# A front in written order, a last projection by output, and means added to x1: one change to a Mamba block with linear attention behind it

## The chip, the cores and the metric

The kernel runs on one core of one Trainium2 chip. A core has five engines that work side by side: TensorE (PE) multiplies matrices into PSUM, VectorE (DVE), ScalarE (ACT) and GpSimd (POOL) work on SBUF and, but for GpSimd, on PSUM, and SyncE (SP) here only issues DMA transfers; ScalarE issues some as well. Each engine takes its instructions in order, and waits on semaphores for the others. The metric is the device time of one execution in microseconds (us). The kernel before takes 7801.51 us, the median of 3 runs (7790.71 to 7805.82).

## The reference

The input `x` is float32, 4 images of 512 channels and 64 x 64 positions (L = 4096). Two layers are added to it:

```python
# layer 0, on gn(x): group norm over 32 groups of 16 channels
xn = layer_norm(xf, norm_g, norm_b)                  # over the 512 channels
chunks = xn cut into 4 blocks of 128 channels, each a sequence of its own
xz = chunks @ in_proj_w.T;  xi, z = split(xz)        # 256 + 256
xc = silu(depthwise_conv4(xi) + conv_b)
dt, Bs, Cs = split(xc @ x_proj_w.T)                  # 8, 16, 16
dt = softplus(dt @ dt_proj_w.T + dt_proj_b)
h[t] = exp(dt*A) * h[t-1] + (dt*xc)[:, None] * Bs    # 256 x 16 states, 4096 steps
y = sum over states of h * Cs + xc * D;  y = y * silu(z)
ym = y @ out_proj_w.T + skip * chunks
x1 = x + layer_norm(ym) @ proj_w.T + proj_b
# layer 1, on gn(x1): linear attention, 8 heads of 64
q, k, v = split(gn(x1) @ w_qkv.T + b_qkv);  q, k = relu(q), relu(k)
kq = sum over positions of k q';  norm = kq.sum + 1e-6
out = x1 + (v kq / norm) @ w_out.T + b_out
```

## The kernel before

**Tiles and steps.** An image is cut into 8 tiles of T = 512 positions, and a tile into 4 chunks of 128 channels: 4 x 8 x 4 = 128 steps (b, t, c). A step makes the projections of its chunk (`inputs`: `pc` for the convolved half through four shifted products with `w_cv`, `pz` for z), `dt`, B and C (`mixers`: `pd`, then `parts`, a bf16 copy of B and C with corrections), the softplus of `dt` (`time_banks`, `time_steps`), and the product `u = dt * xc`. `dt` and `u` (both in one tile `both`, called dt in the profile) are written to DRAM row by row (`to_rows`: `d_rows`) and read back spread out (`spread`: `d_all`), so that 128 partitions hold 4 states of 32 channels: 32 rows, 4 slots `j`, four times over for the states. B is read back as `b_all`, the last 128 columns of C as `c_sb`; the other 384 columns of C are spread by a product with `sel` into PSUM (`c_all`).

**The scan loop.** A step has SLOTS = 16 slots of two scans each. In a slot, GpSimd makes the products `bx = u * B` for two scans (`drive`, L806, two slots ahead), ScalarE the decays `dA = exp(dt * A)` (`decay`, L798, three scans ahead, into three PSUM banks), VectorE the scans (`slot`, L824), every second slot VectorE multiplies the states by C (L844) and GpSimd the last quarter of them (L836), and TensorE sums over the states (`fold_states`). Between them the loop's planner puts the pieces of the next steps' projections, of the next tile's norms (`ahead`), of the tile just scanned (`late`: second norm and projection to x1) and of the attention of the image before (`rest`), each at a slot written by hand or by due times. This loop runs under `tc.manual_schedule()`: its instructions stand in each engine's queue in the order in which the code makes them. What stands before and after the loop is put in order by the framework's own scheduler.

**The front.** Before the loop, ScalarE's queue issues the loads of all weights and biases, `w_pr` (1 MB, the last projection) and `w_qk` (2 MB) among them. Preparations follow in the code: `w_cv` (L234), `dg` (L264), the bias rows `bqk` (L287 to L291), `a_k` and 16 small DMAs on SP that lay it out as `a_t` (L295 to L300), and the folding of the norm's weights into `w_pr`: offsets `pw` (L313), scaling by g (L315), centring by column means (`pw_mean`, L321) and `about` (L331). Then `input_norm(0)`: `stats0` loads the image's 8 tiles into a ring of three buffers (L148) and takes their statistics (L885), `stats_end` makes mean and deviation. `tile_norm(0, 0)` loads the first tile a second time, into `xn` (L519), and applies group norm and layer norm (`normed`, `group_norm`, `layer_norm`). Step 0 then goes through `step_inputs`, `silu`, `mixers`, `time_steps`, `to_rows` and `spread`, step 1 through the first three of these, and the first two products and three decays are made.

**After the loop.** The last tile's projection is `projected_last`: statistics of `ym` by TensorE while the last chunk finishes, 16 products `pp` over 4 outputs `o` and 4 chunks `c` with `c` as the outer loop, and on VectorE for each output the scaling (`sq`, L599), the sum with offset and x (`xr`, L600), its statistics (L603) and their aggregate (L341). The last image's attention follows with nothing beside it: `pq` and `pk` over all positions, then `m2` (`pm` of `w_o` and `kqn`), `m3 = w_v m2 * gr` with the identity added (L1040), the offsets `pob` = m2 bv + m3 ngm with `ngm` the negative group means (and `bo` lessened by `ngm`, since the identity is in m3), and for each tile 16 products `pr = m3 x1`, evicted with the offset `ob` (L1101) and stored. Loaded tiles `xa`, `xb`, `w_o`, `w_v` share one ring of three buffers.

## Time and profile before

| | us |
|---|---|
| median of 3 runs | 7801.51 |
| the profiled execution | 7798.74 |
| its span, first to last instruction | 7797.0 |
| busy: DVE, POOL, PE, ACT | 6968.4, 6892.5, 6424.5, 5442.5 |
| statistics of the first image end (aggregate begins) | 53.4 |
| first product `bx` begins | 114.6 |
| first scan begins | 117.0 |
| last `mv_last` aggregate begins | 7389.8 |
| first product `pr` of the last attention begins | 7678.7 |

A line of a timeline gives the start and the length in us, the engine (SPq and ACTq are their DMA queues, PEld is the loading of TensorE's weights), the line of the code, the operation, what it writes and reads, how often, and in brackets how long the engine had been idle and what released it. Where a helper makes the instruction, its line is the helper's (L129 for all products), and the tile's name tells which it is. One float32 product is two records of TensorE. A table by stretch gives for each stretch the busy time of each engine in turn, then PEclk, the share of full clock granted to TensorE, the DMA engines' busy share, and GB/s.

### The profile page before, as it was taken

The numbers are of one execution on the slowest core, as the hardware profiler recorded it, in microseconds if no ns is written. First come the engines' busy times: TensorE is split into PE (matmuls) and PEld (weight loads), VectorE is DVE, ScalarE is ACT, GpSimd is POOL, SyncE is SP. The second block draws the span as 40 slices with busy tenths as digits, with TensorE's granted clock in tenths as the row PEclk, the third lists the DMA queues.
The fourth block names the chain that finished last, engine by engine and source line by source line (L and its number), as shares of the span: only waits on it lengthen the run. The fifth ranks groups of instructions, "written<-read, shape, count | busy, mean of one in ns | idle before, by whom it ended". The sixth has DMA issues, their size and how long they took to land.

```text
span 7797.0 us, 90419 instructions
## 1 busy us (share of the span) xinstructions
PE 6424.5 (82%) x24816; PEld 2092.9 (27%) x24816; DVE 6968.4 (89%) x5784; ACT 5442.5 (70%) x8289; POOL 6892.5 (88%) x4637
## 2 busy tenths in 40 slices
PE   5677777677789888987788889898788888899699
PEld 1121211111223222332222223332122322333144
DVE  5999999999999999999999999999999999999720
ACT  4667777777777777777777777777777777777421
POOL 4999999999999999999999999999999999999700
PEclk8888888888899999999899999999899999999799
DMA  5666666666666666776766666677666666677402
GB/s 164 165 171 164 158 152 164 162 163 167 173 177 163 162 165 165 181 197 170 174 163 178 177 159 160 165 189 191 162 168 162 159 156 151 159 199 193 126 33 92
DMA packets 829327, 1266.37 MB, mean 162 GB/s; under 512 B 183928, under 2 KB 317576, under 8 KB 816528
## 3 DMA queue, kind: packets, MB, share of 16 engines
q1 hardware_dynamic: 805408, 1223.89, 61.2%
q0 software_dynamic: 16368, 32.51, 2.4%
q8 instruction: 194, 3.18, 0.2%
q10 hardware_dynamic: 7040, 4.20, 0.2%
q14 instruction: 317, 2.60, 0.1%
HBM read 1053.30 MB, written 206.57 MB: 162 GB/s over the span
## 4 chain that ended last, share of the span: by engine, by line
DVE 34%; PE 30%; ACT 10%; DMA 9%; issue 8%; POOL 6%; SPq 3%; DVEq 0%; POOLq 0%; ACTq 0%
DVE h L824 21%; DVE h L844 10%; PE y L129 6%; PE pc L129 6%; PE pq L129 5%; POOL bx L806 5%; DMA d_all<-d_rows 4%; ACT dA L798 3%; PE pr L129 3%; PE po L129 3%; SPq L773 3%; DMA c_sb<-c_rows 2%; PE pp L129 2%; DVE xn L421 2%; PE c_all L129 1%
## 5 line engine op out<-in xcount | busy, mean ns | idle before, releaser
L806 POOL TENSOR_TENSOR bx<-d_all,b_all 128x1024 f32<-128x1024 f32 x2048 | 4824.0, 2367 | 195.2 <-DVE h L824 175.0
L824 DVE TENSOR_TENSOR_SCAN h<-dA,st,bx 128x512 f32<-128x512 f32 x3584 | 4353.8, 1263 | 289.1 <-PE y L129 106.9
L798 ACT ACTIVATE dA<-d_all,a_t 128x512 f32<-128x512 f32 x4096 | 2759.3, 688 | 1503.8 <-DVE h L824 1447.3
L844 DVE TENSOR_TENSOR h<-h,c_all 128x1536 f32<-128x1536 f32 x1024 | 1767.2, 1726 | 0.1
L836 POOL TENSOR_TENSOR h<-h,c_sb 128x512 f32<-128x512 f32 x1024 | 1299.7, 1269 | 97.7 <-DMA c_sb<-c_rows 12.0
L129 PE MATMUL y<-h,fold 128*32 128x512 f32 x8192 | 1264.7, 693 | 50.1 <-POOL h L836 48.4
L129 PE MATMUL c_all<-parts,sel 128*128 128x384 bf16 x1024 | 367.5, 359 | 1021.7 <-DVE h L844 1020.8
L129 PE MATMUL pc<-xn,w_cv 128*128 128x512 f32 x2048 | 1036.5, 640 | 118.8 <-DVE xn L421 57.4
L129 PE MATMUL pq<-w_qk,xa 128*128 128x512 f32 x2048 | 960.2, 604 | 2.5 <-ACT xa L379 2.5
L824 DVE TENSOR_TENSOR_SCAN h<-dA,bx 128x512 f32<-128x512 f32 x512 | 590.3, 1202 | 74.3 <-POOL bx L806 50.9
L129 PEld LDWEIGHTS pc<-xn,w_cv 128*128 128x128 f32 x2048 | 386.4, 199 | 731.2 <-issue 409.5
L129 PEld LDWEIGHTS <-sel 128*128 128x128 bf16 x1216 | 120.3, 99 | 1654.7 <-DVE h L844 1445.6
L129 PEld LDWEIGHTS pq<-w_qk,xa 128*128 128x128 f32 x2048 | 392.7, 195 | 441.7 <-issue 425.9
L129 PE MATMUL pp<-xn,w_pr 128*128 128x512 f32 x1024 | 478.1, 596 | 0.0
L129 PE MATMUL pr<-xb,m 128*128 128x512 f32 x1024 | 476.1, 603 | 2.2 <-ACT res L1101 1.6
L129 PE MATMUL y<-xz,dg 32*32 32x512 f32 x2048 | 357.5, 775 | 0.0
L129 PEld LDWEIGHTS y<-h,fold 128*32 128x32 f32 x8192 | 170.5, 114 | 640.5 <-issue 385.2
L866 POOL TENSOR_TENSOR xz<-xz 128x512 f32<-128x512 f32 x256 | 325.2, 1270 | 8.1 <-ACT xz L863 7.2
L713 POOL TENSOR_TENSOR dt<-dt,xz 128x1024 f32<-128x1024 f32 x128 | 302.2, 2361 | 19.7 <-ACT dt L705 19.7
L129 PE MATMUL pd<-xz,w_xp 128*128 128x512 f32 x512 | 286.9, 687 | 5.2 <-ACT xz L1172 5.2
L129 PE MATMUL pz<-xn,w_z 128*128 128x512 f32 x512 | 270.5, 621 | 7.5 <-ACT xz L692 6.0
L129 PE MATMUL po<-xz,w_op 128*128 128x512 f32 x512 | 258.8, 628 | 5.2 <-POOL xz L866 5.0
(218 smaller groups left out, 5866.8 us busy)
## 6 DMA issues: line engine op xcount, KB each, us to landing
d_all<-d_rows SPq DMA_DIRECT2D x2048, 256.0 KB, 4.4
b_all<-b_rows SPq DMA_DIRECT2D x4096, 64.0 KB, 2.4
d_rows<-dt SPq DMA_DIRECT2D x256, 512.0 KB, 2.8
c_sb<-c_rows SPq DMA_DIRECT2D x4096, 16.0 KB, 3.6
xs<-in_x_dram SPq DMA_DIRECT2D x32, 1024.0 KB, 7.3
xn<-in_x_dram SPq DMA_DIRECT2D x32, 1024.0 KB, 8.3
x<-xr SPq DMA_DIRECT2D x32, 1024.0 KB, 4.3
xa<-x SPq DMA_DIRECT2D x32, 1024.0 KB, 7.0
```

The costliest lines, as they stand in the source:

```text
L129: nc.tensor.matmul(out_, lhsT, rhs, **how)
L421: nc.vector.tensor_tensor(v, v, bc(m, NC), op)
L713: nc.gpsimd.tensor_tensor(f["both"][:, 1], f["both"][:, 0], f["xz"][:, 0], ALU.mult)
L773: nc.sync.dma_start(dst[k * BLK : (k + 1) * BLK, :], rows_[q * KS + k, :].partition_broadcast(BLK))
L798: nc.scalar.activation(dAs[k], fs[n]["d_all", e][:, 0, j, :], AF.Exp, scale=a_t[:, e, j, q : q + 1])
L806: nc.gpsimd.tensor_tensor(bxs[g], fs[n]["d_all", e][:, 1, jj * 2 : jj * 2 + 2, :], bc(b_all[g // JJ], 2), ALU.mult)
L824: nc.vector.tensor_tensor_scan(h[:, j, :], dAs.pop(2 * g + i), bxs[g][:, i, :], 0.0 if t == 0 else st[:, c, e, q, j : j + 1], ALU.mult, AL ...
L836: nc.gpsimd.tensor_tensor(h[:, :, CUT:], h[:, :, CUT:], bc(c_sb.pop(g // JJ), NJ), ALU.mult)
L844: nc.vector.tensor_tensor(own, own, bc(c_all.pop(g // JJ), NJ), ALU.mult)
L866: nc.gpsimd.tensor_tensor(f["xz"][:, 1, e, :], f["xz"][:, 1, e, :], f["xz"][:, 0, e, :], ALU.mult)
```

## The change

The front, from the first weight to the last piece before the loop, now also runs under `tc.manual_schedule()`, so that its instructions stand in written order. Within it:

- The first tile is loaded straight into `xn`; `stats0` takes its statistics there, and `normed` doesn't load it again. `w_pr` and `w_qk` are issued by SP after the eighth x tile.
- The preparations become functions: `w_cv` is made between the statistics of the second and the third tile, the rest after the first group norm; the offsets `pw` are spread over the first tile's norm, and the centring of `w_pr` stands behind the decays.
- The tables of ScalarE's functions are loaded at written places.
- Step 1's `inputs` is begun before step 0's `mixers`. Step 0's softplus, `u`, and rows are made half by half (e = 0, 1); after the first half, `spread` by slot reads `d_all` in sixteen DMAs instead of eight, first the slots 0 and 1 of dt and of u, then 2 and 3. `c_sb` and the second and third `b_all` are issued behind them. Step 1's `mixers` comes after the first decays.

In `projected_last` the products run by output after the first chunk of all four. In the last image's attention the part `m3 ngm` of the offsets is left out; instead VectorE adds `ngm` to each tile of x1, 4 instructions per tile, and then m3 is applied to the sum.

```diff
@@ -164,6 +164,9 @@
+    front = ExitStack()
+    front.enter_context(tc.manual_schedule())
...
@@ -231,7 +234,10 @@
-    nc.vector.tensor_tensor(w_cv, conv_bc, w_x.unsqueeze(1).to_broadcast([P, NTAP, DI]), ALU.mult)
+    def prepare_conv():
+        nc.vector.tensor_tensor(w_cv, conv_bc, w_x.unsqueeze(1).to_broadcast([P, NTAP, DI]), ALU.mult)
...
@@ -269,9 +278,9 @@
-    w_pr = const_rows(proj_w, "w_pr")
+    w_pr = const.tile([P, NC, C], F32, tag="w_pr", name="w_pr")
-    w_qk = const_rows(wqk, "w_qk")
+    w_qk = const.tile([P, NC, 2 * C], F32, tag="w_qk", name="w_qk")
...
@@ -284,51 +293,60 @@
     bv = column(b_qkv[2 * C : 3 * C], NC, "bv")
     bo = column(b_out, NC, "bo")
+    def prepare_bias():
+        nc.vector.tensor_copy(bqk, b_qk)
+        for i in (2, 3):
+            r = slice(i * LANE, P)
+            nc.vector.tensor_tensor(b_qk[r, :], b_qk[r, :], bqk[r, :], ALU.subtract)
+            nc.vector.tensor_copy(bqk[r, :], b_qk[r, :])
     a_t = const.tile([P, NH, NJ, NQ], F32, tag="a_t", name="a_t")
+    def prepare_a():
+        a_k = wk.tile([P, NH, KS, NQ], F32, tag="sq", name="a_k", bufs=4)
+        nc.scalar.activation(a_k, a_sb.rearrange("p e (q k) -> p e k q", k=KS), AF.Exp)
+        nc.vector.tensor_scalar(a_k, a_k, -1.0, None, ALU.mult)
+        for k in range(KS):
+            for j in range(NJ):
+                nc.sync.dma_start(
+                    a_t[k * BLK : (k + 1) * BLK, :, j, :], a_k[j * BLK : (j + 1) * BLK, :, k, :]
+                )
+        nc.vector.tensor_scalar(skd, fold, sk, None, ALU.mult)
+    pw = {}
+    def offset_sums(o):
+        pw[o] = spare_bank(f"pw_{o}", o)
         for c in range(NC):
             mm(
+                pw[o][:, 0:1], w_pr[:, c, o * P : (o + 1) * P], b_sb[:, c : c + 1],
                 start=(c == 0), stop=(c == NC - 1),
             )
+    def offset_take(o):
+        nc.vector.tensor_tensor(pb[:, o : o + 1], pb[:, o : o + 1], pw[o][:, 0:1], ALU.add)
     about = const.tile([P, 1], F32, tag="about", name="about")
+    def scaled():
+        for c in range(NC):
+            nc.vector.tensor_scalar(w_pr[:, c, :], w_pr[:, c, :], g_sb[:, c : c + 1], None, ALU.mult)
+    def centred():
+        pw = work_bank("pw_mean")
+        for c in range(NC):
+            mm(pw, ones.to_broadcast([P, P]), w_pr[:, c, :], start=(c == 0), stop=(c == NC - 1))
+        for c in range(NC):
+            nc.vector.scalar_tensor_tensor(
+                w_pr[:, c, :], pw, -1.0 / C, w_pr[:, c, :], ALU.mult, ALU.add
+            )
+        pw = work_bank("pw_about")
+        for c in range(NC):
+            mm(
+                pw[:, 0:1], ones.to_broadcast([P, P]), b_sb[:, c : c + 1],
+                start=(c == 0), stop=(c == NC - 1),
+            )
+        nc.vector.scalar_tensor_tensor(about, pw[:, 0:1], -1.0 / C, sk, ALU.mult, ALU.mult)
     def stats_tile(name):
...
@@ -516,7 +534,8 @@
     def normed(xn, pad, prev_pad, b, t, norm):
         body = xn[:, :, NTAP - 1 : NTAP - 1 + T]
-        nc.sync.dma_start(body, cols(x, b)[:, :, t * T : (t + 1) * T])
+        if now[0] is not None:
+            nc.sync.dma_start(body, cols(x, b)[:, :, t * T : (t + 1) * T])
         yield from pause(2)
         yield "free"
         if prev_pad is None:
...
@@ -589,12 +608,11 @@
         nc.scalar.activation(rs, rs, AF.Exp, scale=-0.5)
         last = small.tile([P, NC, 1, 6], F32, tag="first", name=f"last_{nm}")
         pps = [spare_bank(f"pp_{nm}_{o}", o) for o in range(NC)]
-        for c in range(NC):
-            for o in range(NC):
-                mm(
-                    pps[o], w_pr[:, c, o * P : (o + 1) * P], ym[:, c, :],
-                    start=(c == 0), stop=(c == NC - 1),
-                )
+        for o, c in [(o, 0) for o in range(NC)] + [(o, c) for o in range(NC) for c in range(1, NC)]:
+            mm(
+                pps[o], w_pr[:, c, o * P : (o + 1) * P], ym[:, c, :],
+                start=(c == 0), stop=(c == NC - 1),
+            )
         for o in range(NC):
             nc.vector.tensor_tensor(sq[:, o, :], pps[o], rs, ALU.mult)
             nc.vector.scalar_tensor_tensor(
...
@@ -715,14 +733,18 @@
         f["d_rows", v] = d_rows
         later(1, lambda: nc.sync.dma_start(d_rows, both[:, v]))
-    def spread(f, e, nm, part):
+    def spread(f, e, nm, part, by_slot=False):
         if part == 0:
             f["d_all", e] = wk.tile([P, 2, NJ, T], F32, tag="d_all", name=f"d_all_{nm}_{e}")
         v, half = divmod(part, 2)
-        src = f["d_rows", v].rearrange("(j i) e t -> i e j t", i=BLK)[:, e]
-        for k in range(half * KS // 2, (half + 1) * KS // 2):
-            nc.sync.dma_start(f["d_all", e][k * BLK : (k + 1) * BLK, v], src)
+        ks, js = range(half * KS // 2, (half + 1) * KS // 2), slice(0, NJ)
+        if by_slot:
+            half, v = divmod(part, 2)
+            ks, js = range(KS), slice(half * NJ // 2, (half + 1) * NJ // 2)
+        src = f["d_rows", v].rearrange("(j i) e t -> i e j t", i=BLK)[:, e, js]
+        for k in ks:
+            nc.sync.dma_start(f["d_all", e][k * BLK : (k + 1) * BLK, v, js], src)
     def mixers(f, nm):
...
@@ -879,8 +901,12 @@
     def stats0(stats, b):
         for t in range(NT):
+            if (b, t) in xn:
+                for c in range(NC):
+                    nc.vector.bn_stats(stats[:, c, t, :], xn[b, t][:, c, NTAP - 1 :])
+                continue
             xt = yield from load_x(b, t, "s")
-            yield
+            yield t if now[0] is None else None
             for c in range(NC):
                 nc.vector.bn_stats(stats[:, c, t, :], xt[:, c, :])
                 if c == NC - 1:
...
@@ -1063,13 +1089,12 @@
         if last:
             banks = [spare_bank(f"pob_{b}_{o}", o) for o in range(NC)]
             nc.vector.tensor_tensor(bo, bo, ngm, ALU.subtract)
-            for v, rhs in ((m2, bv), (m3, ngm)):
-                for o in range(NC):
-                    for p in range(NC):
-                        mm(
-                            banks[o][:, 0:1], v[:, p, o * P : (o + 1) * P], rhs[:, p : p + 1],
-                            start=(v is m2 and p == 0), stop=(v is m3 and p == NC - 1),
-                        )
+            for o in range(NC):
+                for p in range(NC):
+                    mm(
+                        banks[o][:, 0:1], m2[:, p, o * P : (o + 1) * P], bv[:, p : p + 1],
+                        start=(p == 0), stop=(p == NC - 1),
+                    )
             for o in range(NC):
                 offset(o, banks[o])
         for o in range(0 if last else NC):
...
@@ -1104,6 +1129,9 @@
         for t in range(NT):
             x1 = yield from fetched(t, "b")
+            if last:
+                for m in range(NC):
+                    nc.vector.tensor_scalar(x1[:, m, :], x1[:, m, :], ngm[:, m : m + 1], None, ALU.add)
             for o in range(NC):
                 yield from room()
                 pp = work_bank(f"pr_{b}_{t}_{o}")
...
@@ -1143,8 +1171,12 @@
         norms[b] = yield from stats_end(aggregate(stats, f"a{b}"), f"a{b}")
         yield
+    def new_xn(b, t):
+        xn[b, t] = wk.tile([P, NC, NTAP - 1 + T], F32, tag="xn", name=f"xn_{b}_{t}", bufs=3)
     def tile_norm(b, t):
-        xn[b, t] = wk.tile([P, NC, NTAP - 1 + T], F32, tag="xn", name=f"xn_{b}_{t}", bufs=3)
+        if (b, t) not in xn:
+            new_xn(b, t)
         pads[b, t] = small.tile([P, NC, NTAP - 1], F32, tag="pad", name=f"pad_{b}_{t}")
         yield from normed(
             xn[b, t], pads[b, t], pads[b, t - 1] if t else None, b, t, norms[b]
...
@@ -1192,30 +1224,71 @@
             queue.pop(0)
         return False
-    run(input_norm(0))
-    run(tile_norm(0, 0))
+    nc.scalar.preload_act_table_set("natural_log_exp_and_others")
+    new_xn(0, 0)
+    nc.sync.dma_start(xn[0, 0][:, :, NTAP - 1 :], cols(x, 0)[:, :, 0:T])
+    for t in input_norm(0):
+        if t == 2:
+            prepare_conv()
+        elif t == NT - 1:
+            nc.sync.dma_start(w_pr, proj_w.rearrange("(c p) f -> p c f", p=P))
+            nc.sync.dma_start(w_qk, wqk.rearrange("(c p) f -> p c f", p=P))
+    offset_sums(0)
+    wide, taken = 0, []
+    for i, what in enumerate(tile_norm(0, 0)):
+        if i == 2:
+            prepare_d()
+            prepare_bias()
+            prepare_a()
+            offset_take(0)
+        if what == "wide":
+            wide += 1
+            for o in ((1,), (2, 3))[wide - 1]:
+                offset_sums(o)
+        elif wide == 1 and not taken:
+            taken.append(offset_take(1))
+    offset_take(2)
+    offset_take(3)
+    scaled()
+    nc.scalar.preload_act_table_set("silu_and_others")
     run(step_inputs(0))
     silu(0)
-    run(mixers(fs[0], names[0]))
+    nc.scalar.preload_act_table_set("softplus")
+    second = step_inputs(1)
+    for _ in range(2):
+        next(second)
+    first = mixers(fs[0], names[0])
+    next(first)
+    next(first)
     b_row(0)
+    time_banks(fs[0], names[0])
+    for v in range(2):
+        fs[0]["d_rows", v] = dram.tile([P, NH, T], F32, tag=f"d_rows{v}", name=f"d_rows{v}_{names[0]}")
+    for e in range(NH):
+        dt, u = (fs[0]["both"][:, v, e, :] for v in range(2))
+        nc.scalar.activation(dt, fs[0]["pt"][e], AF.Softplus, bias=dtb[:, e : e + 1])
+        nc.gpsimd.tensor_tensor(u, dt, fs[0]["xz"][:, 0, e, :], ALU.mult)
+        for v, row in enumerate((dt, u)):
+            nc.sync.dma_start(fs[0]["d_rows", v][:, e, :], row)
+        if e == 0:
+            for part in range(4):
+                spread(fs[0], 0, names[0], part, True)
     c_tail(0)
-    time_banks(fs[0], names[0])
-    time_steps(fs[0], names[0])
-    for v in range(2):
-        to_rows(fs[0], v, names[0])
-    for part in range(4):
-        spread(fs[0], 0, names[0], part)
+    nc.scalar.preload_act_table_set("silu_and_others")
+    run(second)
+    run(first)
+    c_row(0)
+    silu(1)
+    nc.scalar.preload_act_table_set("natural_log_exp_and_others")
     for g in range(JJ, 3 * JJ, JJ):
         b_row(g)
-    c_row(0)
     for g in range(2):
         drive(g)
-    run(step_inputs(1))
-    silu(1)
-    run(mixers(fs[1], names[1]))
-    nc.scalar.preload_act_table_set("natural_log_exp_and_others")
     for k in range(LEAD):
         decay(k)
+    centred()
+    run(mixers(fs[1], names[1]))
+    front.close()
     with tc.manual_schedule():
         credit, seen, mix, held[0], held_x[0] = 0.0, work["mm"], iter(()), 0, 0
```

Of the hunk at L284 the removed lines are left out: they are the same instructions outside functions, with the offsets one after another.

## The prediction

> **What bounds the kernel now.** I read the page's busy shares and costliest groups first, then the front's waits and timeline (to 125 us), then the timeline and clock of the end (from 7318 us).
>
> ```profile
> PE 6424.5 (82%) x24816; PEld 2092.9 (27%) x24816; DVE 6968.4 (89%) x5784; ACT 5442.5 (70%) x8289; POOL 6892.5 (88%) x4637
> ...
> L806 POOL TENSOR_TENSOR bx<-d_all,b_all 128x1024 f32<-128x1024 f32 x2048 | 4824.0, 2367 | 195.2 <-DVE h L824 175.0
> L824 DVE TENSOR_TENSOR_SCAN h<-dA,st,bx 128x512 f32<-128x512 f32 x3584 | 4353.8, 1263 | 289.1 <-PE y L129 106.9
> ```
>
> From about 115 to 7360 us VectorE and GpSimd run the scan loop side by side, each idle little: the loop sets some 93% of the time. The compiled instructions of the two kernels stand in the same order on every engine from the first scan's slot to the last projection, so the loop is not edited. The change works before and after it.
>
> The waits of SP's queue in the first 60 us (total, times, longest):
>
> ```profile
> SPq L148 <- DVE st L885: 17.9, 4, 9.9
> SPq L148 <- DMA w_xp<-in_xp_w_dram: 10.1, 1, 10.1
> ```
>
> The eight x tiles are loaded in eight calls, but they stop twice for long: once for a weight load with which they share only a completion semaphore (SP's and ACT's DMAs take eight of them in turn), and for VectorE, which had put preparations between the statistics that free a tile. The timeline (start, length, engine, instruction, idle time before it):
>
> ```profile
> 53.40 1.04 DVE L341 BATCH_NORM_AGGREGATE mv_a<-st 128x2 f32<-128x48 f32 x4
> ...
> 58.27 1.52 ACT L379 ACTIVATE xn<-xn,off_a,gr_a 128x512 f32<-128x512 f32 x2 [16.56 <-DMA a_t<-a_k]
> ...
> 86.74 1.28 ACT L1172 ACT_TABLE_LOAD   x1
> ...
> 114.58 9.25 POOL L806 TENSOR_TENSOR bx<-d_all,b_all 128x1024 f32<-128x1024 f32 x4 [16.41 <-DMA d_all<-d_rows]
> ...
> 116.95 5.82 DVE L824 TENSOR_TENSOR_SCAN h<-dA,bx 128x512 f32<-128x512 f32 x5 [40.58 <-POOL bx L806]
> ```
>
> Statistics end at 53.4, the norm starts at 58.27, and the first scan waits for the first product, which waits until 2 MB of `d_all` have landed. At the end TensorE and then VectorE are the path:
>
> ```profile
> 7382.13 0.69 DVE L599 TENSOR_TENSOR sq<-pp,rs 128x512 f32<-128x512 f32 x1 [19.06 <-PE pp L129]
> ...
> 7389.82 0.30 DVE L341 BATCH_NORM_AGGREGATE mv_last<-last 128x2 f32<-128x6 f32 x2
> ```
> ```profile
> 7669.32 4.34 PE L129 MATMUL pob<-bv,w_o 128*128 128x1 f32 x32
> ...
> 7673.53 5.26 PE L129 MATMUL pob<-ngm_b,m 128*128 128x1 f32 x24
> 7678.65 2.06 PE L129 MATMUL pr<-xb,m 128*128 128x512 f32 x2
> 7680.49 1.71 PE L129 MATMUL pob<-ngm_b,m 128*128 128x1 f32 x8
> ...
> 7682.06 18.35 PE L129 MATMUL pr<-xb,m 128*128 128x512 f32 x38
> ```
>
> **Step 1, loads and statistics: -16 us.** `w_pr` and `w_qk` (3 MB) go from ACT's queue in the middle of the x loads to SP's behind them; the reload of the first tile (1 MB, issued at 42.3) is gone, since that tile is now read straight into `xn`; VectorE does only `w_cv` (1.23) between statistics. So four tiles are issued at 0.8 to 2.2 us. With `conv_bc`, `w_x` and `w_z` that is 5 MB, at the 370 GB/s of the busy slices 13.5 us: the fourth lands near 16. The other four still wait for small loads whose semaphore they inherit. The last `w_xp` (issued near 11.7, 3.8 to land) lets the fifth go at 16. ACT's `dtb` can now only be issued when the fourth x tile is in (16.2); `b_sb` follows at 17.9 and takes up to the 8.8 it took, I say 7: the sixth goes at 25. `pb` (22 plus 5.5) and `b_qk` (23 plus 2.5) let the last two go at 27.5 and 28. At 2.7 us per MB and 2 for the landing the last is in at 35; its four statistics (0.68 each) end at 37.5, against 53.4. Ends: 33 if the small loads land as fast as the 3.4 of `bv`, 44 if each takes 8.8. ACT's last DMA goes at about 28, ahead of the norm; the 16 `a_t` issues on SP (10.3 us) now follow the norm, and have the 35 us until `b_rows`.
>
> **Step 2, norm to first scans: -5 us.** I put the new order onto the old clock, norm at 58.27. Four groups of eight one-column products `pw` (1.74 us each by the old row: 32 in 6.96) now lie in TensorE's queue: before the mean sums (hidden), before the variance sums (1.44 us of gap: +0.3) and two before `pc` (3.0 of gap for 3.5: +0.5). VectorE gets 3.6 us of bias and `a_k` work after the norm, inside the 5.3 it waits for the mean; were that gone, up to 3.6. The silu table load (1.28) moves ahead of the `pc` evictions, under TensorE's 10 us. Against that, `pd` now stands behind half of the next step's `pc` (eight records of 0.43): it starts at 91.2, not 89.6. Then `dt` copied 93.8, softplus by half to 95.8 and 96.8, first half's product on GpSimd 97.1 (1.27), `d_rows` of that half issued at 97.2 and 97.7, first `d_all` at 99.7 (before: 100.17).
>
> Here is the gain: of 16 `d_all` DMAs of 128 KB the first eight are what the first product needs. The trace moved 2.1 MB of `d_all` and 0.46 of `b_all` from 100.2 to 114.5, with slices of 180 to 230 GB/s; half of it is in at about 105.5, and the first product ends at 107.9 (before: 116.9). The Trainium skill speaks against this (DMA: Bandwidth & Descriptors, Anatomy of one DMA): about 2 us fixed per DMA, twice as many of them now, and 436 GB/s beyond, measured there on GpSimd's path. At that rate the old 2.1 MB would have been in at 107, the split would be worth 2.5 us and ACT, whose decays can start at 106.4, would bind. I take the row.
>
> What is late next: the doubled DMAs are queued in front of `c_sb` and the second `b_all` on SP. Second-half `d_all` lands at 110, so the second product ends at 112.4; `b_all` lands at 114, the third ends at 116.4 and the fourth at 118.7 (before: 123.8). VectorE's centring of `w_pr` (2.5) stands ahead of the first scan and waits for `pw_mean`, behind `c_all` on TensorE: it ends at 109.7, so the first two scans start 1.8 after their product, and are still done when the second product is. That is what hides it; without it, 1.8. Left over: 5.1 of the 9. Ends: 2 (`d_all` no faster per half) and 8.
>
> **Step 3, loop: 0.** Shifted as it stands. Nothing in the trace shows how it reacts to another start; I take 6 either way.
>
> **Step 4, last projection: -3.** Sixteen products either way, 22 of 32 records in a row from 7374.96 to 7384.4. Column by column all four outputs finish in the last 3 us, and VectorE's chain (about 1.85 per output) starts at 7382.1. By output the first is ready at 7376.7 and the chain keeps up (2.6 per output on TensorE): only the last output's sq, xr, stats and aggregate (0.69, 0.73, 0.68, 0.15 and waits) follow 7384.5, ending 7387.0 instead of 7390.1. Ends 2 and 4.
>
> **Step 5, last attention: -7.4.** 16 products (32 records) of m3 with the mean go. From 7673.53 to 7682.06 that is 8.5 us, of which the `pr` pair would be needed anyway: 1.9, so 6.6. The 32 added VectorE instructions cost 0.42 each (the `w_pr` scaling by a column, four in 1.67), 1.7 per x1 tile, under 13.9 us of products per tile. The first tile's stand ahead of two copies of m2 that the m3 products wait for: x1 is issued at 7644.79 and landed in 4.7, three adds end near 7650.8, the copy was due at 7653.0. Landing in the 10.0 that is the longest of this row would cost 3. And the clock (PE busy, then PEclk in the column after POOL):
>
> ```profile
> 7665.00:7670.00 5.00, 5.00 (x18) 2.58 (x17) 0.73 (x4) 1.16 (x2) 0.00 (x0) 1.00 0.00 0
> 7670.00:7675.00 5.00, 5.00 (x34) 5.00 (x34) 0.73 (x4) 0.21 (x1) 0.00 (x0) 0.70 0.79 236
> 7675.00:7680.00 5.00, 5.00 (x20) 4.46 (x21) 0.00 (x0) 0.00 (x0) 0.00 (x0) 0.50 0.45 184
> 7680.00:7685.00 5.00, 5.00 (x13) 2.95 (x12) 0.63 (x4) 0.00 (x0) 0.00 (x0) 0.50 0.00 0
> 7685.00:7690.00 5.00, 5.00 (x12) 2.09 (x12) 0.00 (x0) 0.69 (x1) 0.00 (x0) 0.93 0.13 52
> ```
>
> One-column products fill TensorE's row, and the granted clock still falls to half 3 us into them, and stays there for 4 us of wide ones. The Trainium skill (TensorE: Matmul & The Clock Gate, Part 1) ties the half clock to an idle window of 3.4 us: an engine busy throughout would stay at full clock, and the gain would be 6.6. By the row, eight wide records at half clock cost 2.7 us, and a shorter one-column phase saves 0 to 2.7 of them. It still exceeds 3 us, so I take 0.8.
>
> **Sum.** 16 + 5 + 0 + 3 + 7.4 = 31.4. The profiled span of 7797.0 becomes 7765.6; 1.7 lie around it (7798.74), and the median of the runs is 2.8 above that run: 7801.5 - 31.4 = 7770.
>
> **Rivals.** (a) *Small loads hold the x stream.* Four tiles ahead of ACT's column loads keep them at 8.8 us or worse, statistics end at 46 or later: 8 us lost, 7778 to 7784. For it: the 10.1 us wait above. Against it: 3 MB less compete. (b) *The front's gain is swallowed.* The first steps of the loop run to the pace of `d_all` and `c_sb` (in the chain to 260 us `d_all` has 16%, in the whole 4%); if that catches up, only steps 4 and 5 are left: 7791. Against it: SP's `b_all` and `c_sb` issues in the loop wait above all for GpSimd (L773, 1124.7 us behind its `st` copy), which moves with the start. (c) *Slower: the loop settles into another phase.* Its scans idle 289 us, 2.3 per step of 128; if each step waits longer for one landing, 0.25 us per step cancels everything, 0.37 makes it slower by 0.2%, and 0.5 gives 7834. Against it: same order, and lanes of semaphores already differ from step to step. (d) *The loop gains from it instead*, 0.1 us per step: 7757.
>
> **How the numbers follow.** As worked out 0.67, (a) 0.13, (b) 0.09, (c) 0.06, (d) 0.05. A difference under 0.2%, 15.6 us, can hardly be told from none: as worked out, (a) and (d) are faster by more (0.85), (b) is within (0.09), (c) slower (0.06). The range: low from step ends 20, 8, 4, 9.3 not all at once, 45 in all: 7756; high from (a) with step 2 at its poor end, 7788; it leaves out (b) and (c).
>
> **What would show it.** Aggregate near 37.5; first product near 90 with `d_all` still as its releaser; the loop's GpSimd and VectorE groups at the same means and idle times; last `mv_last` 3 us after the last `pp`; no `pob<-ngm`, `pr` in one piece, at half clock for its first 3 to 4 us. Wrong if statistics end after 46, if products two and three wait longer than the first gained, or if the loop's idle times change by over 30 us.

## The result, and the profile after

The changed kernel takes 7780.18 us, the median of 8 runs (7776.45 to 7788.46), beside 7802.15 us of the kernel before in 8 runs (7790.71 to 7812.5). The ratio is 0.9974, with a 95% interval of 0.9963 to 0.9985: by the ratio 20 us faster, 12 to 29; the two medians lie 22.0 us apart. The predicted 7770 was 10 us too low. The profiled execution took 7786.57 us with a span of 7784.8, 6.4 us above the median of its runs; beside the span of 7797.0 before that is 12.2 us.

The page of the changed kernel has the same three groups in front (busy time, mean of one in ns, idle time before it and what ended most of it):

```profile
PE 6430.9 (83%) x24784; PEld 2088.4 (27%) x24784; DVE 6983.2 (90%) x5816; ACT 5442.9 (70%) x8288; POOL 6897.0 (89%) x4638
...
L828 POOL TENSOR_TENSOR bx<-d_all,b_all 128x1024 f32<-128x1024 f32 x2048 | 4826.9, 2369 | 204.4 <-DVE h L846 187.5
L846 DVE TENSOR_TENSOR_SCAN h<-dA,st,bx 128x512 f32<-128x512 f32 x3584 | 4354.7, 1264 | 305.6 <-PE y L129 111.8
```

The products and scans cost what they cost before (2367 and 1263 ns), but the scans idle 305.6 us instead of 289.1 and the products 204.4 instead of 195.2. That is the first sign that the loop did not simply move in time.

SP's waits in the first 60 us (total, times, longest), and the timeline of the front:

```profile
SPq L148 <- DMA w_xp<-in_xp_w_dram: 14.6, 1, 14.6
SPq L148 <- DMA b_sb<-in_norm_b_dram: 5.9, 1, 5.9
...
SPq L148 <- DVE st L911: 0.5, 1, 0.5
```
```profile
38.66 1.04 DVE L359 BATCH_NORM_AGGREGATE mv_a<-st 128x2 f32<-128x48 f32 x4
...
43.53 1.52 ACT L397 ACTIVATE xn<-xn,off_a,gr_a 128x512 f32<-128x512 f32 x2 [15.94 <-POOL xn L542]
...
89.71 2.36 POOL L828 TENSOR_TENSOR bx<-d_all,b_all 128x1024 f32<-128x1024 f32 x1 [7.92 <-DMA d_all<-d_rows]
...
90.32 2.48 DVE L340 SCALAR_TENSOR_TENSOR w_pr<-pw_mean,w_pr 128x512 f32<-128x512 f32 x4 [27.50 <-PE pw_mean L129]
...
94.34 2.35 POOL L828 TENSOR_TENSOR bx<-d_all,b_all 128x1024 f32<-128x1024 f32 x1 [2.27 <-DMA d_all<-d_rows]
...
97.29 4.65 POOL L828 TENSOR_TENSOR bx<-d_all,b_all 128x1024 f32<-128x1024 f32 x2 [0.61 <-DMA b_all<-b_rows]
```

VectorE no longer holds the x tiles back (0.5 us instead of 17.9); small loads do, for 20.5 us. (Before, beside the 10.1 us for `w_xp` that the prediction lists, the same view had 5.3 us for `dpar` and 1.1 for `w_dt`.) The statistics end 14.7 us earlier than before, and so does the norm start. The first product starts 24.9 us earlier, but the third and fourth wait for `b_all`; the fourth ends at 101.9 instead of 123.8. So the front gained 21.9 us in this pair.

At the end of the kernel:

```profile
7373.02 9.61 PE L129 MATMUL pp<-xn,w_pr 128*128 128x512 f32 x22
...
7375.03 0.69 DVE L617 TENSOR_TENSOR sq<-pp,rs 128x512 f32<-128x512 f32 x1 [13.91 <-PE pp L129]
...
7384.90 0.18 DVE L359 BATCH_NORM_AGGREGATE mv_last<-last 128x2 f32<-128x6 f32 x1
```
```profile
7644.37 1.28 DVE L1134 TENSOR_SCALAR xb<-xb,ngm_b 128x512 f32<-128x512 f32 x3 [0.44 <-DMA xb<-x]
...
7664.03 4.43 PE L129 MATMUL pob<-bv,w_o 128*128 128x1 f32 x32
...
7668.32 22.11 PE L129 MATMUL pr<-xb,m 128*128 128x512 f32 x45
```

VectorE starts on the first output 2.0 us after the first `pp` record instead of 7.2, and the last aggregate ends 12.1 us after it instead of 15.2: 3.1 us. `pob<-ngm` is gone, and `pr` starts right behind the 32 records of m2. From the end of the last scan product to the end of the span it is 431.8 us instead of 442.1.

So the two ends gained 21.9 + 10.3 = 32.2 us in a pair whose spans differ by 12.2. The loop between them gave 20 us back. Following each of the 2048 products in both traces shows where: the changed kernel is 21.9 us ahead at product 576 (2,088 us), 8.9 ahead at product 832, and 8.0 ahead at product 1152; it falls to 1.6 behind by product 1408 and ends the loop 1.95 ahead. In no other of the stretches looked at does the distance change by more than 4 us.

### The profile page after: what moved, and what is told of

Read it like the earlier page. It is cut to its first block, busy times and chain, and to the rows that moved or that the text cites. A ratio compares the mean times of both kernels' runs of the same rounds, so it can differ in the third digit from the quotient of the medians.

```text
span 7784.8 us, 90406 instructions
## 1 busy us (share of the span) xinstructions
PE 6430.9 (83%) x24784; PEld 2088.4 (27%) x24784; DVE 6983.2 (90%) x5816; ACT 5442.9 (70%) x8288; POOL 6897.0 (89%) x4638
## 3 DMA queue, kind: packets, MB, share of 16 engines
q1 hardware_dynamic: 806352, 1225.99, 60.3%
q8 instruction: 194, 3.18, 0.2%
## 4 chain that ended last, share of the span: by engine, by line
DVE 36%; PE 33%; ACT 10%; issue 7%; DMA 6%; POOL 5%; SPq 2%; DVEq 0%; POOLq 0%; ACTq 0%
DVE h L846 23%; DVE h L866 11%; PE y L129 6%; PE pc L129 6%; PE pq L129 6%; POOL bx L828 4%; ACT dA L820 4%; PE pr L129 3%; PE po L129 3%; PE pp L129 2%; DMA d_all<-d_rows 2%; DMA c_sb<-c_rows 2%; DVE xn L439 2%; SPq L795 2%; PE c_all L129 1%
## 5 line engine op out<-in xcount | busy, mean ns | idle before, releaser
L828 POOL TENSOR_TENSOR bx<-d_all,b_all 128x1024 f32<-128x1024 f32 x2048 | 4826.9, 2369 | 204.4 <-DVE h L846 187.5
L846 DVE TENSOR_TENSOR_SCAN h<-dA,st,bx 128x512 f32<-128x512 f32 x3584 | 4354.7, 1264 | 305.6 <-PE y L129 111.8
L858 POOL TENSOR_TENSOR h<-h,c_sb 128x512 f32<-128x512 f32 x1024 | 1301.4, 1271 | 97.2 <-DMA c_sb<-c_rows 11.5
L888 POOL TENSOR_TENSOR xz<-xz 128x512 f32<-128x512 f32 x256 | 325.7, 1272 | 12.1 <-ACT xz L885 9.7
L857 POOL COPY st<-h 128x4 f32<-128x4 f32 x1024 | 210.3, 205 | 59.0 <-DVE h L846 54.4
```

The lines of the kernel that those rows point to most:

```text
L828: nc.gpsimd.tensor_tensor(bxs[g], fs[n]["d_all", e][:, 1, jj * 2 : jj * 2 + 2, :], bc(b_all[g // JJ], 2), ALU.mult)
L846: nc.vector.tensor_tensor_scan(h[:, j, :], dAs.pop(2 * g + i), bxs[g][:, i, :], 0.0 if t == 0 else st[:, c, e, q, j : j + 1], ALU.mult, AL ...
L857: nc.gpsimd.tensor_copy(st[:, c, e, q, :], h[:, :, T - 1])
L858: nc.gpsimd.tensor_tensor(h[:, :, CUT:], h[:, :, CUT:], bc(c_sb.pop(g // JJ), NJ), ALU.mult)
L888: nc.gpsimd.tensor_tensor(f["xz"][:, 1, e, :], f["xz"][:, 1, e, :], f["xz"][:, 0, e, :], ALU.mult)
```

## The experiments

The theories: *sum* (the parts add up, the loop keeps any gain, and what it gave back in the first pair is chance), *give-back* or *start* (the loop is longer when it starts earlier), and *content* (something else in the new front makes it longer). In the expectations, *tied to the front* is the theory that the front decides which length the loop has. Since the loop turned out to vary, each run is split in the same way, from its own trace: the column *start* is the time at which the fourth product `bx` ends, *loop* goes from there to the end of the last product, *end* is the rest of the span. The last column is the time from the end of product 1152 to the end of product 1408, with the number of 3.41 us windows in it in which TensorE had half its clock.

| kernel | start | loop | end | median of runs (n) | 1152 to 1408 |
|---|---|---|---|---|---|
| before | 123.8 | 7231.1 | 442.1 | 7802.15 (8) | 928.0 (25) |
| before, again | 123.1 | 7238.1 | 442.0 | 7801.38 (13) | 928.0 (25) |
| tails alone | 120.9 | 7233.0 | 431.9 | 7791.71 (21) | 928.0 (25) |
| changed | 101.9 | 7251.0 | 431.8 | 7780.18 (8) | 937.5 (33) |
| changed, again | 103.4 | 7247.6 | 431.8 | 7777.22 (7) | 937.5 (33) |
| front alone | 103.6 | 7241.1 | 442.0 | 7791.34 (21) | 937.5 (33) |
| d_all whole | 104.7 | 7242.5 | 431.8 | 7780.69 (8) | 937.5 (33) |
| w_pr, w_qk on ACT | 109.4 | 7244.3 | 431.8 | 7782.16 (10) | 928.0 (25) |
| lanes as before | 102.9 | 7250.5 | 431.8 | 7781.7 (19) | 937.5 (33) |
| pause of 40 | 116.2 | 7236.7 | 432.0 | 7788.46 (20) | 931.4 (28) |
| pause of 60 | 122.7 | 7243.1 | 431.7 | 7794.66 (13) | 934.8 (33) |
| two edits more | 96.4 | 7240.8 | 428.4 | 7766.15 (5) | 928.3 (29) |
| two edits more, again | 97.3 | 7243.9 | 428.6 | 7771.48 (5) | 928.0 (25) |

A profile is one execution; where its span stands to the median of its kernel's runs differs (1.75 us lie around a span).

### The changed kernel again

No edit.

> The changed kernel itself, once more. In the first pair of profiles the front is 21.9 us earlier, and still 22 us earlier at 2,090 us, then the loop gives back 13 us between 2,090 and 2,780 us and 10.6 us between 4,130 and 4,950 us, where half-clock stretches of TensorE are longer than before. Theory 'chance' (the 3.41 us windows of the clock fall otherwise on the same work in each execution): this profile gives back another amount at other places, and over more runs the difference from before goes towards 22 + 10 = 32 us (7770). Theory 'give-back' (the shifted loop pays for it): the same stretches lose about 20 us again, and the difference stays near 22 us (7780).

Measured: 7777.22 us (7 runs, 7775.57 to 7787.9), ratio 0.9973 (0.9962 to 0.9984). The loop is longer than before again, by 16.5 us against the first profile of before. The stretch from product 1152 to 1408 took the very same 937.5 us; the stretch from 576 to 832, where the first pair lost 13 us (930.4 against 917.3), took 918.9 this time. So one of the two losses is not a property of the kernel. The difference did not go to 32 us, as *chance* alone would have it.

### Front and tails, each alone

Front alone: the changed kernel with the last projection and the last attention of before.

```diff
-for o, c in [(o, 0) for o in range(NC)] + [(o, c) for o in range(NC) for c in range(1, NC)]:
-    mm(pps[o], ...)
+for c in range(NC):
+    for o in range(NC):
+        mm(pps[o], ...)
...
-            for o in range(NC):
-                for p in range(NC):
-                    mm(banks[o][:, 0:1], m2[...], bv[:, p : p + 1], ...)
+            for v, rhs in ((m2, bv), (m3, ngm)):
+                for o in range(NC):
+                    ...
...
-            if last:
-                for m in range(NC):
-                    nc.vector.tensor_scalar(x1[:, m, :], x1[:, m, :], ngm[:, m : m + 1], None, ALU.add)
```

Tails alone: the same three pieces put the other way into the kernel before.

> The front of the change alone; last projection and last attention as before. Theory 'sum' (parts add up, the loop keeps what the front gains): 21 to 22 us under the kernel before (7780). Theory 'give-back' (the loop returns some 10 us of any front gain): 12 us under it (7790).

> The last projection by output and the mean added to x1 alone; front as before. The prediction's steps 4 and 5: 10.4 us under the kernel before (7791), whatever the loop does with the front. Theory that the tail's gain is smaller than the pair of profiles says (clock of the end luckier after): 6 us.

Measured: front alone 7791.34 us (21 runs), ratio 0.9986 (0.9979 to 0.9992): 11 us under before, 6 to 16. Tails alone 7791.71 us (21 runs), ratio 0.9991 (0.9985 to 0.9998): 7 us under it, 2 to 12. (By the medians, beside 7799.9 for the runs of before next to them, both are 8 to 9 us under it.) In their profiles the front's start is 19.5 to 20.3 us earlier than in the two profiles of before (17.3 us earlier than in that of tails alone, which has the old front too), and the end of the tails 10.1 to 10.2 us shorter. The tails pay in the time what the trace shows, within the interval. The front does not: some 9 of its 20 us are missing (of 17, some 6). This is where the prediction's 10 us are.

### Pauses in front of the loop

```diff
 scaled()
+for _ in range(10):            # 15 in the second
+    for c in range(NC):
+        nc.vector.tensor_scalar(xn[0, 0][:, c, :], xn[0, 0][:, c, :], 1.0, None, ALU.mult)
```

> The changed kernel with 40 more VectorE instructions (the first tile times 1.0, 0.42 to 0.5 us each, 17 to 20 us together) between the norm and the first step's products, so that the loop starts later by that. Theory 'sum': 17 to 20 us above the changed kernel (7798). Theory 'give-back': the loop takes back about half, 8 to 10 us above it (7789).

> The changed kernel with a pause of 60 VectorE instructions, by the 12.8 us of 40 some 19.2 us, so that the fourth first product ends near 122, where the old front has it. Theory 'content' (something in the new front other than its start makes the loop some 8 us longer): start and tails as in the kernel with the old front and the new tails, but the loop still longer: 7799 to 7800. Theory 'start' (the loop is longer because it starts earlier): the time of the old front with the new tails, 7792 to 7794. Theory 'chance': the same 7799 or less, with any pattern of half clock.

Measured: the 40 instructions delayed the fourth product by 12.7 us beside the second profile of the changed kernel and 14.2 beside the first, less than the 17 to 20 expected. The time rose to 7788.46 us (20 runs, 7779.01 to 7803.46): 8 us over the changed kernel's first median, 11 over its second. With 60 instructions the fourth product ends at 122.7, as with the old front, and the time is 7794.66 us (13 runs, 7787.16 to 7821.46), ratio to before 0.9997 (0.9988 to 1.0005). *Start* asked for 7792 to 7794, *content* for 7799 to 7800. As a time 7794.66 is nearer to the first; by the ratio it is 2 us under before, where tails alone is 7 under it and *content* asks for about none, which is nearer to the second. The interval of some 13 us holds both, so these times do not settle it. Nor is the pause only a later start: it also puts 40 or 60 more instructions into VectorE's stream, which matters below.

### Semaphores and buffers of the loop as before

```diff
 nc.sync.dma_start(w_qk, ...)
+spare = new_tile("spare")
+free_x()
+for i in range(7):
+    part = (slice(None), i // 2, slice(i % 2 * T // 2, (i % 2 + 1) * T // 2))
+    nc.sync.dma_start(spare[part], cols(x, 0)[:, :, 0:T][part])
```

The new front issues another number of DMAs, so every DMA in the loop has another of the eight completion semaphores, and every x tile another of the three buffers. Seven more small loads and one more buffer turn both back: in the traces all 10,697 DMAs that SP issues in the loop have the semaphore of before again, and in the changed kernel none of them has.

> The changed kernel with one more x buffer taken and seven small x loads into it (0.9 MB, read by nobody) behind w_qk, so that every DMA of the loop has the completion semaphore and every x tile the buffer that it has in the kernel before. Theory 'content' in its nearest form (the turn of semaphores and buffers makes the loop longer): 8 us under the changed kernel, 7771. Every other theory: as the changed kernel, 7777 to 7781, with 0 to 2 us for the extra bytes.

Measured: 7781.7 us (19 runs), ratio 0.9974 (0.9967 to 0.9981), loop 7250.5, and the stretch from 1152 to 1408 took 937.5 again. Which semaphore and which buffer the loop has makes no difference. *Content* in this form falls.

### The kernel before again

> The kernel before, once more with a profile. In products 1152 to 1408 of the scan loop (about 4,130 to 5,060 us) the two profiles with the old front took 928.0 us with 25 half-clock windows, the three with the new front 937.5 with 33, the one with the new front and a pause 931.4 with 28. Theory 'tied to the front': 928 again. Theory 'chance': any of these. The first products' ends tell whether the front of the profiled run (fourth product at 123.8 us) was typical: the one with the old front and new tails had it 3.4 us earlier.

Measured: 7801.38 us (13 runs), ratio 1.0002 (0.9994 to 1.001); fourth product at 123.1, so the profiled front was typical; 928.0 us with 25 windows. All three profiles with the old front have that length to 0.1 us.

### What the half clock does in the loop

Both traces have, near product 1152, the same stop of TensorE: `c_all` waits 3.05 us for VectorE. The timeline of TensorE there, and a table in stretches that follow the clock's own windows (PE busy first, then PEclk after POOL), in the kernel before:

```profile
4152.32 0.34 PE L129 MATMUL c_all<-parts,sel 128*128 128x384 bf16 x1 [3.05 <-DVE h L844]
```
```profile
4149.50:4152.90 3.40, 0.58 (x5) 0.25 (x9) 3.40 (x3) 2.24 (x4) 3.32 (x5) 1.00 0.79 266
4152.90:4156.30 3.40, 3.40 (x18) 0.45 (x12) 3.40 (x4) 1.84 (x3) 3.40 (x2) 0.50 1.12 224
4156.30:4159.70 3.40, 2.90 (x8) 0.83 (x8) 3.40 (x4) 3.35 (x5) 3.32 (x5) 1.00 0.98 298
```

and in the changed kernel:

```profile
4144.91 0.50 PE L129 MATMUL c_all<-parts,sel 128*128 128x384 bf16 x1 [3.05 <-DVE h L866]
```
```profile
4140.70:4144.10 3.40, 1.16 (x3) 0.19 (x1) 3.40 (x4) 2.92 (x6) 3.32 (x4) 1.00 0.90 288
4144.10:4147.50 3.40, 2.59 (x13) 0.50 (x17) 3.40 (x4) 1.19 (x3) 3.40 (x3) 0.50 1.11 248
4147.50:4150.90 3.40, 3.40 (x12) 0.50 (x4) 3.40 (x5) 2.42 (x3) 3.32 (x3) 0.50 0.99 242
4150.90:4154.30 3.40, 3.40 (x6) 1.33 (x5) 3.40 (x3) 3.10 (x4) 3.40 (x4) 0.50 0.97 177
4154.30:4157.70 3.40, 3.40 (x20) 0.80 (x19) 3.36 (x4) 3.40 (x6) 3.40 (x2) 1.00 0.26 59
```

The clock changes only on a grid of 3.413 us, and the grid does not start with the program: a grid line lies 2.28 us after the start of the span before, 0.31 after it in the changed kernel, and elsewhere in the other profiles. The Trainium skill (TensorE: Matmul & The Clock Gate, Part 1) says the same, a free-running window of 3413 ns that isn't reset by a kernel. In the kernel before the stop lies almost wholly in one window and costs one window of half clock. In the changed kernel a grid line cuts it, and it costs three. The same page has one busy window suffice for the return to full clock. In the kernel before one did; in the changed kernel the third window was still at half after one that was busy throughout.

Between products 1152 and 1408 (attention of the image before beside the scans) TensorE is busy some 220 of 250 us, so a lost window is felt there: with 25 windows the stretch takes 928.0 us, with 33 it takes 934.8 to 937.5. That is up to 1.2 us for each window more, of the 1.7 that half a clock takes from it. Over all 13 profiles, loops with the old front take 7231 to 7238 us, mean 7234; the eight with the new front and no pause 7241 to 7251, mean 7245. Of these 11 us, 6 lie in products 1152 to 1408 and 3 in products 576 to 832, the other such stretch.

That the lengths come back to 0.1 us has a reason: the loop falls into step with the grid. This is where each profile stands on the grid, in us after a grid line, when a product ends:

| end of product | 4 | 576 | 960 | 1152 | 1408 |
|---|---|---|---|---|---|
| three with the old front | 1.28 to 3.18 | 0.05 to 1.67 | 1.48 | 0.64 to 0.66 | 0.21 to 0.22 |
| five with 937.5 us | 0.01 to 2.07 | 0.16 to 2.22 | 1.48 to 1.49 | 1.45 to 1.47 | 0.31 to 0.32 |
| other five | 0.25 to 1.63 | 0.06 to 0.41 | 1.48 to 1.50 | 0.37 to 0.66 | 0.18 to 0.22 |

At product 960 all thirteen stand at the same place, whatever their start. From there to product 1408 they take 1603.0, 1606.4, 1609.8 or 1613.3 us, each some 3.4 us, or one window, more than the one before it. So a gain in the front, or a delay on the way, arrives at such a place in whole windows or not at all.

Where the five leave the others can be seen too: at one scan of VectorE, soon after product 1143. Counted from product 1024, all profiles but one (the first of two edits more) stand within 0.1 us of each other in the twelve products up to it. The scan in the kernel before and in the changed one:

```profile
4106.63 1.28 DVE L824 TENSOR_TENSOR_SCAN h<-dA,st,bx 128x512 f32<-128x512 f32 x1 [0.35 <-ACT dA L798]
```
```profile
4098.21 1.28 DVE L846 TENSOR_TENSOR_SCAN h<-dA,st,bx 128x512 f32<-128x512 f32 x1 [0.68 <-POOL dt L731]
```

Its decay `dA` ends at the same point of the loop in both. The scan starts 0.10 to 0.11 us behind it before and in seven more profiles, but 0.44 to 0.46 us behind it in all five profiles with 937.5 us. (The `dt` in the bracket isn't what it waits for: in the other eight the scan starts before that product is done.) These 0.35 us have become 0.8 us at product 1152, and the grid then cuts the stop of TensorE in two: three windows, 10.3 us from product 960 to 1408.

What makes the scan late is, as far as the traces tell, its place in VectorE's own stream. In the five it has 4,415 instructions of VectorE before it in the trace, waits for semaphores included; with the old front 4,420, in the kernels with `w_pr` on ACT and two edits more 4,417, with the pauses 4,455 and 4,475. And in all 13 traces there are 19 places behind VectorE's first 150 instructions at which it sat idle and then started over 0.07 us later than the last event that it waited for. Every one of them has 63 instructions more than a multiple of 128 before it (4,415 is 34 x 128 + 63); the old front has none of the 19. The profile's page of the kernel before suggests why 128:

```profile
q8 instruction: 194, 3.18, 0.2%
q14 instruction: 317, 2.60, 0.1%
```

These are the queues that bring in instructions. Together they moved 5.78 MB in an execution of 90,419 instructions, 64 bytes for each, and a packet of q14 has 8,192 bytes in the trace: by this estimate 128 instructions. That a scan at the seam of two such pieces starts late is an inference from this; no packet arrives just at the late scan, and no run changed VectorE's count and nothing else.

So in this stretch the traces speak for *content*, in a form that the run with the old semaphores did not touch, and against *start*: the pattern with 937.5 us is missing with a start that is later (pauses, `w_pr` on ACT) and with one that is earlier (two edits more), and all of these have another count. The times do not follow the start either. Worked out from the start and end of each profile, with 122.6 and 442 for before, the loop takes back 8 to 11 us by the ratio in the five kernels with the pattern and 4 to 8 in the other five with the new front, with starts from 96 to 123 us and an interval of 5 to 11 us either way for each. That the kernels without the pattern lose so much too is not explained: for the rest of the loop, products 576 to 832 above all (919 and 930 us in the same kernel), the cause stays open.

### d_all whole

```diff
-                spread(fs[0], 0, names[0], part, True)
+                spread(fs[0], 0, names[0], part)
```

> The changed kernel with the first d_all spread as before the change (one DMA per repeat with both slots, eight fewer descriptors lists of half the size), so that the first product needs all of dt and u. Step 2 by the trace: in the changed kernel's profile the four first products start at 89.7, 94.3 and 97.3 us and end at 101.9; undone, the first starts when the last d_all lands, near 96.5, and four at 2.36 us end near 106: 4 us later. By the rule on DMA[...]: all of d_all is in by about 92 to 93, the fourth ends at 101 to 102: nothing lost. The time moves by no more than that (7779 to 7783).

GpSimd and VectorE in the timeline:

```profile
95.47 9.25 POOL L828 TENSOR_TENSOR bx<-d_all,b_all 128x1024 f32<-128x1024 f32 x4 [13.22 <-DMA d_all<-d_rows]
...
97.84 5.82 DVE L846 TENSOR_TENSOR_SCAN h<-dA,bx 128x512 f32<-128x512 f32 x5 [2.80 <-POOL bx L828]
```

The first product starts 5.8 us later than in the first profile of the changed kernel, but the fourth ends at 104.7, 1.3 to 2.8 us later. Counted from the first `d_all` issue, the fourth product ends after 23.7 us before, 21.2 with `d_all` whole in the new order, 19.0 and 19.3 in the two profiles with halves. So the halves are worth about 2.1 us. Another 2.4 are left for the rest of the new order (`c_sb` and the second `d_rows` now follow `d_all`); no run tested that part alone, and tails alone, which has the old order, needed 22.1, so it may be as little as 0.9. The time, 7780.69 us (8 runs, ratio 0.9974, 0.9964 to 0.9984), can't show 2 us.

### w_pr and w_qk on ACT's queue

```diff
-    w_pr = const.tile([P, NC, C], F32, tag="w_pr", name="w_pr")
+    w_pr = const_rows(proj_w, "w_pr")
...
-    w_qk = const.tile([P, NC, 2 * C], F32, tag="w_qk", name="w_qk")
+    w_qk = const_rows(wqk, "w_qk")
...
-            nc.sync.dma_start(w_pr, ...)
-            nc.sync.dma_start(w_qk, ...)
```

> The changed kernel with the loads of w_pr and w_qk (3 MB) on ACT's queue again, in the middle of the small loads. Step 1: 3 MB at 370 GB/s in front of the last x tiles are 8 us, the statistics end at 46 to 47 instead of 38.7, the time is up to 8 us more (7787). Rival (the stream is held by the semaphores of small loads and not by bytes): 1 to 3 us.

```profile
SPq L148 <- DMA w_dt<-in_dt_w_dram: 14.7, 1, 14.7
SPq L148 <- DMA dpar<-in_d_par_dram: 4.6, 1, 4.6
```
```profile
44.12 1.04 DVE L359 BATCH_NORM_AGGREGATE mv_a<-st 128x2 f32<-128x48 f32 x4
```

The statistics end 5.5 us later (aggregate at 44.12, not 38.66), the fourth product at 109.4, 6.0 to 7.5 us later; 8 were expected from the bytes, 1 to 3 by the rival. The x tiles wait for small loads for about as long as without the 3 MB (20.4 us with a third, shorter wait; 20.9 in the changed kernel), so the bytes are what is left to account for the loss. The time is 7782.16 us (10 runs, ratio 0.9978, 0.9969 to 0.9987), 2 to 5 us over the changed kernel's two medians, which is less than the start lost; this kernel has the 928.0 us pattern.

### Two edits more

(1) The 21 small loads behind `cb` go on SP's queue behind `w_pr`. (2) The m2 products with `bv` go among the m3 products.

```diff
+    waiting = []
+    def small_load(*what):
+        waiting.append(what)
 ...                             # w_xp, w_dt, dtb ... bo: small_load(...) for nc.scalar.dma_start(...)
             nc.sync.dma_start(w_pr, ...)
+            for what in waiting:
+                nc.sync.dma_start(*what)
             nc.sync.dma_start(w_qk, ...)
...
             taken.append(later(1, lambda m=m, pm=pm: take3(m, pm)))
+            for o in {0: (0, 1), 1: (2, 3)}.get(m, ()) if last else ():
+                banks.append(spare_bank(f"pob_{b}_{o}", o))
+                for p in range(NC):
+                    mm(banks[o][:, 0:1], m2[:, p, o * P : (o + 1) * P], bv[:, p : p + 1],
+                        start=(p == 0), stop=(p == NC - 1))
             yield
```

> The changed kernel with two edits meant to be better than both. (1) The 21 small loads behind cb go on SP's queue after w_pr, so no x tile shares a semaphore with one: if step 1's reading of the waits is right, the fifth to eighth x tile wait for their buffers alone, the statistics end at 30 to 32 us instead of 38.7, and the first products move with them, 6 to 8 us. If the stream is bound by bytes or by VectorE, 0 to 3. (2) The 16 one-column products m2 x bv stand among the m3 products instead of behind them: if the half clock comes from one-column products alone in TensorE's window, the first pr products run at full clock (res 1.5 to 2.5 us earlier); if it comes from the idle stretch before, no change. Together 7769 to 7772.

> The kernel with the small loads on SP's queue and the one-column products among the m3 products once more, for its interval: 5 runs had 7766.15 (7757 to 7774). Start 6.6 and end 3.4 us earlier than the changed kernel make 7769; if the loop keeps returning some of an earlier start, 7772.

SP's waits up to 60 us and the timeline, then the stretches of the last attention (PE busy first, PEclk after POOL):

```profile
SPq L148 <- DVE st L916: 9.3, 4, 3.0
SPq L148 <- DMA xs<-in_x_dram: 8.2, 1, 8.2
```
```profile
32.26 1.05 DVE L364 BATCH_NORM_AGGREGATE mv_a<-st 128x2 f32<-128x48 f32 x4
```
```profile
7640.00:7645.00 5.00, 5.00 (x25) 3.30 (x24) 0.75 (x6) 0.69 (x1) 0.00 (x0) 1.00 0.00 0
7645.00:7650.00 5.00, 5.00 (x13) 2.15 (x12) 1.40 (x9) 0.69 (x1) 0.00 (x0) 1.00 0.00 0
7650.00:7655.00 5.00, 5.00 (x13) 2.22 (x12) 0.73 (x4) 0.69 (x1) 0.00 (x0) 1.00 0.39 126
```

No x tile waits for a small load any more, only for its buffer and for x itself; the statistics end at 33.3 and 34.2 in the two profiles instead of 39.3 to 39.7, and the fourth product at 96.4 and 97.3. So the small loads held the x stream, for some 5 to 6 us. At the end, two groups of 16 one-column records (1.84 us each) between wide products leave the clock at 1.00, where the same 32 in a row were followed by half clock (tables in the next section); the end is 3.3 us shorter, more than the 1.5 to 2.5 expected. The edit only moves these records, and two windows of half clock are 3.4 us of lost clock: that is the gain. The times are 7766.15 us (5 runs, ratio 0.9954, 0.994 to 0.9967) and 7771.48 us (5 runs, ratio 0.9961, 0.9948 to 0.9974): faster than before, by the medians of the runs beside them 28 to 33 us; the changed kernel's two medians are 6 to 14 us higher, in runs of another time, and no interval was taken for that.

## Why the prediction was right and where it was wrong

The direction, the range and the two ends were right; the middle was wrong.

**Step 1 (-16): -14.5.** The aggregate ends at 39.2 to 39.7 in the profiles of the changed kernel, with or without its tails or a pause, beside 53.5 and 54.4 before. The mechanism, small loads whose semaphore an x tile inherits, is shown by the two edits more: without them the stream ends 5 to 6 us earlier. (In the trace the fifth tile's DMA has the semaphore of the last `w_xp`, the sixth's that of `b_sb`.) The waits for `w_xp` (14.6) and `b_sb` (5.9) are the two that the step named; rival (a), 8 us lost to them, did not come.

**Step 2 (-5): -5.2 and -7.2, by another split.** From norm to the fourth product it is 58.4 and 60.3 us, not 65.6. But the step put 5.1 us on the halves, and they are worth 2.1; the row that was taken said more than the rule set against it: the 2.5 us estimated from the page's figures (Trainium skill, DMA: Bandwidth & Descriptors, Anatomy of one DMA) are nearer to what was measured. The trace shows what limits it: the third and fourth product wait for `b_all`, which lies behind the doubled DMAs on SP, as the step had foreseen. The rest came with what the step had not priced: the order behind `d_all` (2.4 or less, as said above) and an issue 0.8 to 2.5 us earlier, of which it had counted 0.5. That these made up for what the halves lacked is luck. The centring stood ahead of the first scan as predicted, and VectorE did not hold up the second product.

**Step 3 (loop 0, "I take 6 either way"): +8 to +11. This is the step that failed.** By the times the loop gives back about 9 of the front's 20 us (11 left, 6 to 16), by the profiles 11. The step took the loop as unedited because its instructions stand in the same order on every engine. The order did stay, and yet the loop did not: the new front leaves VectorE at another place in its instruction stream, one scan starts 0.35 us late in the changed kernel, as far as the traces tell for that reason, and the grid of the clock makes three windows of it (10.3 us in products 960 to 1408, in the five kernels where that scan is late). The rest stays open. The bound of 6 was not drawn from anything; the half-clock windows, which step 5 had before its eyes in the same profile, could have given one: 8 windows more in one stretch of 256 products are 9.5 us. The reason given against rivals (b) and (c), that order and semaphores don't matter, holds for the semaphores (the run with the lanes of before). Rival (b) was right by half as to size, for a reason that isn't its own: the loss is not in the first steps (products 4 to 128 take 422.6 to 427.2 us in all profiles, old or new) but 2,000 us later and more. Rival (c), a loop that settles into another phase, had the right word, but not the mechanism: no landing in each step, but a few places where the clock loses whole windows.

**Step 4 (-3): -3.1.** As worked out: the chain keeps up with the products, and only the last output's part follows them.

**Step 5 (-7.4): -7.1.** One-column products still fill TensorE's row and still bring the half clock. Two tables of 5 us, in the columns as above:

```profile
7660.00:7665.00 5.00, 5.00 (x20) 2.68 (x18) 0.73 (x4) 1.37 (x2) 0.00 (x0) 1.00 0.00 0
7665.00:7670.00 5.00, 5.00 (x26) 4.14 (x27) 1.90 (x10) 0.00 (x0) 0.00 (x0) 0.66 0.82 239
7670.00:7675.00 5.00, 5.00 (x9) 2.10 (x8) 2.63 (x7) 0.41 (x1) 0.00 (x0) 0.65 0.43 180
```

Two windows of half clock are left of four (6.8 us instead of 13.7). So 3.4 us of the 7.1 are clock, where the step had 0.8: its 6.6 for the records came from a row that lay in half clock itself, and only the sum was right. The step's row against the rule on idle windows was decided rightly: TensorE is busy throughout and loses the clock all the same.

**Sum.** 19.5 to 20 from the front instead of 21, 10.2 from the end instead of 10.4, and 9 given back instead of none: 20 to 21, as measured by the ratio. The 9 are themselves worked out from the time of the front alone. The result stayed inside the range because the range was wide for other reasons: step 3 had no term for what happened. Its low end does not add up as stated, either: the four step ends named there make 41.3 us together, not 45.

## What to carry to other kernels

When a front gets shorter, don't book its gain until the loop has been compared product by product in both traces, and on the clock's grid; here the clock took a part back 2,000 us and more behind the edit, and 256 products of one and the same kernel differed by 11.5 us between two executions. Instructions in the same order are not the same loop: their place in the engine's stream can differ as well. Price the half clock from the profile like any other cost: count its windows in each stretch, and keep one-column stretches of TensorE short, between wide products. A split into halves brings only what the next thing in the queue lets through: price the fourth product, not the first. And loads that share nothing with each other but a completion semaphore belong behind the stream that matters.

## What the runs showed of the hardware

- The clock of TensorE moves on a grid of 3.413 us that is free of the program. The same stop of 3.05 us cost one window of half clock in the kernel before and three in the changed one, where the grid cut it otherwise.
- Beside scans and attention the loop falls into step with that grid: at product 960 all 13 profiles stand 1.48 to 1.50 us behind a grid line, and from there to product 1408 they take 1603.0, 1606.4, 1609.8 or 1613.3 us, steps of one window.
- VectorE started late, by up to 0.4 us, at 19 places in 13 profiles, and each stands 63 behind a multiple of 128 in its stream as the trace counts it; one of them, 0.35 us late, ends as three windows.
- 32 one-column records in a row (4.4 us) brought two windows of half clock behind them, and two groups of 16 (1.84 us each) between wide products none.
- An x tile waited 14.6 us for the landing of a weight load (`w_xp`) with which it shared only the semaphore.
